# State-space loop of a small hybrid network: a step's two projections as one block product of seven half-width products, SiLU as one function, and the steps reordered

## The chip, the cores and the metric

The kernel runs on 1 core of one Trainium2 chip. The metric is the time of the kernel on the device in microseconds (us). A core has a matrix engine (TensorE, PE in the profile, with its weight loads as PEld), VectorE (DVE), ScalarE (ACT), GpSimd (POOL) and SyncE (SP), which here only issues transfers (DMA). TensorE writes into PSUM, which is split into eight banks of 512 float32 columns; the other data lie in SBUF, 128 partitions wide. All arithmetic that concerns us is in float32.

## The reference: what is computed

The input x has 2 batches of 512 tokens of width 512 (1024 tokens in eight tiles of 128). Six blocks follow each other: a gated feed-forward layer with 4-bit weights, a state-space layer, the feed-forward layer again, a small memory layer, attention, and the memory layer again. The change is in the state-space layer. Cut to what matters, with 128 heads of 64 channels, 8 groups of heads, 128 states, and chunks of 128 tokens:

```python
h = x * rsqrt(mean(x * x) + EPS) * norm_w
proj = einsum('bsd,od->bso', h, in_proj_w)          # 8192 gate, 8192 hid, 1024 B, 1024 C, 128 dt
gate, hBC, dt = split(proj)
hBC = silu(causal_conv(hBC, conv_w, conv_b))        # four taps along the tokens, by channel
hid, B, C = split(hBC)
dt = softplus(dt + dt_bias); A = -exp(A_log)
# by chunk: M = (C . B) * exp(segsum(A * dt)); Y_diag = M @ (hid * dt)
# states carried from chunk to chunk; Y_off = (C * exp(cumsum)) . state before the chunk
y = Y_diag + Y_off + Dp * hid
yg = y * silu(gate)
yg = yg * rsqrt(mean over the group (yg * yg) + EPS) * gnorm_w
out = x + einsum('bsd,od->bso', yg, out_proj_w)
```

## The kernel before

**The steps.** The 8192 channels are taken 128 at a time (two heads, one "pair"), for one batch of 512 tokens. A group of heads has 8 pairs. A step is (g, b, q): group, batch, pair in the group; b changes after eight q, g after both b. So there are 128 steps, and the loop in `ssm` calls `period(n)` for n = 0 to 129. One period works on three steps at once: the projections and convolution of step n (`cur`), the state-space sums of step n-1 (`p1`), and the output projection of step n-2 (`p2`).

**What one period does on TensorE, by its name in the profile and its line:** the projection of hid, cp_h, four products of 128 x 128 by 128 x 512 (L883, called from `period`); the chunks' states st of p1 (L1078); the output product po of p2, four chunks into four PSUM banks that add up over the eight q (L1000); py of p1, the products with M (L1160) and with the carried states (L1169); the gate's projection pg (L883); and ht, four transposes of hid (L1213). In the trace a float32 product counts as two instructions.

**The other engines.** VectorE: the taps 2 to 4 of the convolution (`conv_taps`, L897), the product with SiLU's second half (`silu`, L906: SiLU is built as (tanh(x/2) + 1) * x, with the convolution's weights halved beforehand), hc = hid * dt (L1021), two scans that make the decays within a chunk (L974, one for each head), their product with C·B (L988), the carried states (L1088), and yg (L1176, L1180). ScalarE: first tap (L892), Tanh of hid (L902) and of the gate (L1017), six scalings hd (L1029), two Exp over the scans (L979, L1125), the square of yg (L1186), the scaling of the output weights (L1191). GpSimd: Cs, C times the decay since the chunk's start (L990, 768 columns), and the sum of squares ssum (L1187).

**Work that comes once in eight steps.** B and C of the next group or batch are projected and convolved at q = 5 and q = 6 (`group_b`, `group_c`), B is transposed into Btok (L945, L947) and C·B is formed (L954, L958). When a group and batch is through, pr (L1108) sums the squares over channels, ScalarE takes the root (L1113), and four chunks of po are scaled on ScalarE (L1148) and added to x on GpSimd (L1150). In periods 1 to 7 `setup_later` also prepares dt and the decays of batch 1.

**What sets the order.** Inside the loop the order on TensorE, VectorE, ScalarE and GpSimd is the order in which the program is written (`in_order`); SP's transfers are placed by the scheduler. The program waits wherever two engines touch the same tile; for a PSUM tile that holds for two readers as well. A bank that is used again waits for its last reader.

**PSUM in the loop:** four banks for po, and one each for "tr" (ht, then st, bt, cb, pr), "mm" (pg, B, C), "dd" (cp_h) and "y" (py).

**Transfers.** Weights of the projections are 256 KB tiles (128 x 512 float32) from a pool of 20; they are loaded at b = 0 and kept for b = 1. Each step loads rows, 1024 KB, the decays of two heads broadcast to all partitions (L966).

Of the kernel before, what the change touches and what calls it, by code (L numbers as in the profile page):

```python
# [18 lines left out]
P = 128  # L19
# [33 lines left out]
OT_HID, OT_B, OT_C, OT_DT = NPT, 2 * NPT, 2 * NPT + NG, 2 * NPT + 2 * NG  # L53
# [213 lines left out]
class Kernel:  # L267
    def __init__(self, tc, ctx, a, out):
# [13 lines left out]
        self.eps = self.const.tile([P, 2], F32, name="eps")  # L282
        nc.vector.memset(self.eps[:, 0:1], EPS)
        nc.vector.memset(self.eps[:, 1:2], 4.0 * EPS)
# [12 lines left out]
    def ssm_const(self):  # L297
        with (
            self.tc.tile_pool(name="ssm_const", bufs=1) as pool,
            self.tc.tile_pool(name="early", bufs=1) as self.early,  # L300
        ):
            self.sc = pool
            self.small = pool.tile([P, 80 * 5 + 2 * NPT + KD], F32, name="small")
            self.later = pool.tile([P, S], F32, name="later")
            self.bias = pool.tile([P, 2, NH], F32, name="bias")
            yield
# [30 lines left out]

    def w2(self, src, name):
# [5 lines left out]
    def norm_parts(self, tag, each=None, gain=None, lazy=False):  # L344
# [15 lines left out]
        def root(t, to):  # L360
            nc.scalar.activation(
                rstd[:, t:to], mv[:, t:to, 1], AF.Sqrt, bias=self.eps[:, 0:1]
# [57 lines left out]
    def unpack_in(self, pool, which, ht):  # L420
# [10 lines left out]
        wt = self.wpool.tile([P, KD, P], F32, tag="w", name=f"w{which}_{ht}")  # L431
# [4 lines left out]
        return wt  # L436
# [27 lines left out]
    def ffn(self, n, then=None, during=None):  # L464
# [10 lines left out]
        def weight(which, ht):  # L475
            if first:
                t = (
                    self.unpack_out(pool, ht)
                    if which == 2
                    else self.unpack_in(pool, which, ht)  # L480
                )
# [6 lines left out]
            load = self.w2 if which == 2 else self.w  # L488
# [18 lines left out]
        def sums(ht):  # L507


            w1, w3 = weight(1, ht), weight(3, ht)  # L510
            lo, hi = slice(0, 2), slice(2, 4)
            if ht:
                s, u = (
                    self.wpool.tile([P, KD, P], F32, tag="w", name=f"ws{i}{n}_{ht}")
                    for i in range(2)
                )
# [174 lines left out]
    def ssm(self, hT, start, turn):  # L691
        tc, nc = self.tc, self.nc
        self.hT, self.start, self.turn = hT, start, turn
        with ExitStack() as ctx:
            self.sp = ctx.enter_context(tc.tile_pool(name="ssm", bufs=1))
            ctx.enter_context(self.banks("psum_s", tr=1, po=4, dd=1, mm=1, y=1))
            ctx.enter_context(self.in_order())
            self.steps = [
                Step(g, b, q) for g in range(NG) for b in range(NB) for q in range(PAIRS)
            ]  # L700
            self.wo = {}
# [3 lines left out]
    def ssm_norm(self):  # L705
# [9 lines left out]
        nc.vector.tensor_scalar(  # L715
            out=small[:, :400], in0=small[:, :400], scalar1=0.5, scalar2=None, op0=ALU.mult
        )
        ms = self.sc.tile([P, NT], F32, name="ms")

        def each(t, h):  # L720
# [4 lines left out]
            nc.scalar.activation(m, m, AF.Sqrt, bias=self.eps[:, 0:1], scale=1.0 / D)  # L725
# [8 lines left out]
    def dt_z(self, b):  # L734
        nc, (z, e, o) = self.nc, self.zeo
        bs = slice(b * NC, (b + 1) * NC)
        pz = self.ps("y", [P, NC, NH], f"pz{b}")
# [84 lines left out]
    def ssm_setup(self, t, ht, hT):  # L822

        nc = self.nc
        if (t, ht) == (NC + 1, 1):
            self.hT = hT
            self.gw, self.sh, late = {}, {}, []
# [10 lines left out]
            self.wdt = self.w(self.a["w_in"][OT_DT], "wdt")  # L838
# [6 lines left out]
            for first, taps, end in late:  # L845
                first()
                taps()
                end()
        elif (t, ht) == (NC + 1, NHT - 1):
# [12 lines left out]
    def setup_later(self, n, part):  # L862


        for at, f, *args in (
# [5 lines left out]
            ((5, 2), self.decay, "start", "tr"),  # L871
            ((5, 3), self.row, 0, "tr"),
            ((6, 2), self.row, 1, "tr"),
            ((6, 3), self.decay, "dt_end", "tr"),
            ((7, 2), self.decay, "whole", "tr"),
# [12 lines left out]
    def first_tap(self, p, ct, name):  # L888

        w = self.convw[:, ct, :]  # L890
        acc = self.early.tile([P, S], F32, tag="acc", name=f"acc_{name}", bufs=2)
        self.nc.scalar.activation(acc, p, AF.Identity, bias=w[:, 4:5], scale=w[:, 3:4])  # L892
        return p, w, acc, name

    def conv_taps(self, p, w, acc, name):
        for s in range(1, 4):
            self.nc.vector.scalar_tensor_tensor(  # L897
                out=acc[:, s:], in0=p[:, : S - s], scalar=w[:, 3 - s : 4 - s],
                in1=acc[:, s:], op0=ALU.mult, op1=ALU.add,
            )  # L900
# [996 lines left out]
```

## Time and profile before

| | us |
|---|---|
| time, median of 3 runs | 2763.68 (2761.5 to 2764.07) |
| span of the profiled execution | 2762.9 |
| TensorE busy | 2683.4 |
| VectorE busy | 1999.1 |
| ScalarE busy | 1110.3 |
| GpSimd busy | 522.8 |

The profile is of one execution, whose own time is its span from the first to the last instruction; the three times are of other executions. A row of groups reads: line, engine, operation, tile written and tiles read, shape, how many; then busy us and mean ns of one; then the engine's idle time ahead of these instructions and what ended it. A timeline row reads: start in us, length in us, engine, line, operation, tiles, how many in a row; in brackets the idle time before it and its releaser. A waits row reads: who waited for whom, us in all, times, longest. An instruction's own length can hold a wait too: Cs is between 1.80 and 2.75 us long, a scan between 1.19 and 2.81.

The loop's ht transposes start at 258.3 us for the first step and at 2098.5 us at the last row of that line. In the window from 250 to 2107 us TensorE is busy for 1847 of 1857 us, VectorE for 1496, ScalarE for 830, GpSimd for 482; the granted clock is 1.00 and the DMA share 0.29.

### The profile page before, as it was taken

What the parts mean: (1) busy time and instruction counts of PE and PEld (TensorE: products, weight loads), DVE (VectorE), ACT (ScalarE), POOL (GpSimd) and SP (SyncE); (2) the same over time, 40 slices, a digit from 0 to 9 for tenths busy, and PEclk for the clock granted to TensorE, in tenths of its full rate; (3) what the DMA queues carried; (4) which work ended last, traced back from release to release, by engine and by line L of the source; (5) the groups of instructions that cost most, each with busy time, mean ns of one, the idle gap of its engine ahead of it and who ended that gap; (6) DMA issues with size and microseconds to landing.
All of it is one profiled execution on the core that took longest, in us unless ns stands there. A gap on an engine that the chain in (4) does not pass through costs nothing.

```text
span 2762.9 us, 33381 instructions
## 1 busy us (share of the span) xinstructions
PE 2683.4 (97%) x12208; PEld 1395.9 (51%) x12208; DVE 1999.1 (72%) x3622; ACT 1110.3 (40%) x2428; POOL 522.8 (19%) x344
## 2 busy tenths in 40 slices
PE   8999999999999999999999999999999999889897
PEld 4445555555555555555555555555555444445443
DVE  7845877878778788787878878778886532665555
ACT  2214443444444344444444434444443211344443
POOL 0001122323223222231322312323130000110000
PEclk9999999999999999999999999999999999889988
DMA  7623133223323322322332332232221110000000
GB/s 205 199 98 114 69 107 132 90 77 130 107 84 116 110 84 96 124 92 87 129 100 80 116 125 84 84 130 96 84 99 50 31 54 23 0 1 2 1 1 31
DMA packets 75619, 237.76 MB, mean 86 GB/s; under 512 B 9824, under 2 KB 10400, under 8 KB 58944
## 3 DMA queue, kind: packets, MB, share of 16 engines
q1 hardware_dynamic: 70416, 226.00, 23.9%
q10 hardware_dynamic: 4752, 8.65, 0.8%
q8 instruction: 97, 1.59, 0.2%
q0 software_dynamic: 288, 0.98, 0.1%
q14 instruction: 66, 0.54, 0.1%
HBM read 223.80 MB, written 11.80 MB: 85 GB/s over the span
## 4 chain that ended last, share of the span: by engine, by line
PE 86%; DVE 8%; ACT 4%; issue 1%; POOL 0%; DMA 0%; SPq 0%; ACTq 0%; DVEq 0%; POOLq 0%
PE po L1000 15%; PE pg L883 14%; PE cp_h L883 13%; PE fo L669 5%; PE fmm L502 5%; PE py L1160 4%; PE st L1078 3%; PE py L1169 3%; PE fy L502 2%; PE cp_CT L883 2%; PE cp_BT L883 2%; PE ht L1213 2%; DVE acc_h L897 1%; PE w L1667 1%; PE fdd L502 1%; PE av L1683 1%
## 5 line engine op out<-in xcount | busy, mean ns | idle before, releaser
L883 PE MATMUL pg<-hT_s,wi 128*128 128x512 f32 x1024 | 474.3, 606 | 0.0
L1000 PE MATMUL po<-wo,yg 128*128 128x512 f32 x1024 | 460.7, 593 | 0.5 <-DVE yg L1180 0.5
L883 PE MATMUL cp_h<-hT_s,wi 128*128 128x512 f32 x1024 | 460.6, 592 | 0.0
L974 DVE TENSOR_TENSOR_SCAN M<-rows,later 128x512 f32<-128x512 f32 x256 | 431.7, 1725 | 0.0
L1187 POOL TENSOR_TENSOR ssum<-ssum,sq 128x512 f32<-128x512 f32 x112 | 142.4, 1271 | 1215.7 <-ACT sq L1186 1215.7
L897 DVE SCALAR_TENSOR_TENSOR acc_h<-cp_h,small,acc_h 128x511 f32<-128x511 f32 (+2 forms) x384 | 286.4, 746 | 21.3 <-ACT acc_h L892 12.2
L883 PEld LDWEIGHTS pg<-hT_s,wi 128*128 128x128 f32 x1024 | 184.6, 190 | 206.8 <-issue 204.2
L1000 PEld LDWEIGHTS po<-wo,yg 128*128 128x128 f32 x1024 | 184.8, 190 | 184.4 <-issue 183.6
L883 PEld LDWEIGHTS cp_h<-hT_s,wi 128*128 128x128 f32 x1024 | 184.6, 190 | 183.6 <-issue 183.6
L990 POOL TENSOR_TENSOR Cs<-CT,rows 128x768 f32<-128x768 f32 x128 | 252.5, 1972 | 18.7 <-PE py L1169 16.0
L902 ACT ACTIVATE th_h<-acc_h 128x512 f32<-128x512 f32 x128 | 80.7, 630 | 348.3 <-DVE acc_h L897 342.6
L1029 ACT ACTIVATE hd<-ht,end 128x64 f32<-128x64 f32 x768 | 171.1, 324 | 44.5 <-DVE hc L1021 44.4
L1186 ACT ACTIVATE sq<-yg 128x512 f32<-128x512 f32 x112 | 70.6, 630 | 284.2 <-DVE yg L1180 284.2
L988 DVE TENSOR_TENSOR M<-M,CB 128x512 f32<-128x512 f32 x256 | 166.2, 686 | 12.4 <-ACT M L1125 12.3
L1021 DVE TENSOR_TENSOR hc<-ht,dt 128x512 f32<-128x512 f32 x128 | 88.1, 689 | 115.5 <-PE ht L1213 115.5
L1088 DVE SCALAR_TENSOR_TENSOR st<-st,whole,st 128x64 f32<-128x64 f32 x512 | 108.8, 274 | 65.5 <-ACT st L1083 65.5
L979 ACT ACTIVATE M<-M 128x512 f32<-128x512 f32 x128 | 80.7, 630 | 169.6 <-DVE M L974 169.6
L1631 DVE CUSTOM_DVE_ANT_0 j<-s,future 128x384 f32<-128x384 f32 (+3 forms) x256 | 112.8, 487 | 46.2 <-PE s L1621 46.0
L1160 PEld LDWEIGHTS py<-M,hc 128*64 128x64 f32 x2048 | 109.4, 136 | 68.2 <-issue 64.7
L1160 PE MATMUL py<-M,hc 128*64 128x128 f32 x2048 | 140.5, 279 | 1.1 <-DVE M L988 1.1
L1078 PEld LDWEIGHTS st<-hd,Btok 128*128 128x128 f32 x768 | 104.1, 191 | 69.7 <-issue 41.3
L906 DVE SCALAR_TENSOR_TENSOR v<-v,pg 128x512 f32<-128x512 f32 x128 | 87.3, 682 | 48.5 <-ACT v L1017 47.8
(330 smaller groups left out, 3762.1 us busy)
## 6 DMA issues: line engine op xcount, KB each, us to landing
rows<-rows SPq DMA_DIRECT2D x128, 1024.0 KB, 4.7
wi<-in_w_in_dram SPq DMA_DIRECT2D x144, 256.0 KB, 2.8
wo<-in_w_out_dram SPq DMA_DIRECT2D x64, 256.0 KB, 3.0
keep<-w ACTq DMA_DIRECT2D x33, 256.0 KB, 3.7
wk<-keep SPq DMA_DIRECT2D x33, 256.0 KB, 2.7
wi<-in_q_dram SPq DMA_DIRECT2D x44, 128.0 KB, 3.1
sc<-in_s_dram SPq DMA_DIRECT2D x44, 128.0 KB, 3.2
wi<-in_q_dram SPq DMA_DIRECT2D x11, 256.0 KB, 3.3
```

The source lines that it names most:

```text
L502: nc.tensor.matmul(dst, lhsT=w[:, k, :], rhs=x[:, k, :], start=start and k == 0, stop=stop and k == 1, skip_group_check=True,)
L669: nc.tensor.matmul(po, lhsT=act[ht][:, b, c * P : (c + 1) * P], rhs=w2[ht], start=ht == 0, stop=ht == NHT - 1,)
L883: self.nc.tensor.matmul(p, lhsT=wt[:, k, :], rhs=self.hT[b][:, k, :], start=k == 0, stop=k == KD - 1)
L897: self.nc.vector.scalar_tensor_tensor(out=acc[:, s:], in0=p[:, : S - s], scalar=w[:, 3 - s : 4 - s], in1=acc[:, s:], op0=ALU.mult, op1=ALU ...
L974: self.nc.vector.tensor_tensor_scan(out=m, data0=rows[:, i, 0, :], data1=self.later, initial=0.0, op0=ALU.add, op1=ALU.mult,)
L988: self.nc.vector.tensor_tensor(out=m, in0=m, in1=sh["CB"], op=ALU.mult)
L990: self.nc.gpsimd.tensor_tensor(out=cur.Cs, in0=sh["CT"][:, P:].unsqueeze(1).to_broadcast([P, 2, S - P]), in1=cur.rows[:, :, 1, P:], op=ALU ...
L1000: self.nc.tensor.matmul(self.po[c], lhsT=p2.yg[:, c * P : (c + 1) * P], rhs=self.wo[p2.ct], start=p2.q == 0, stop=p2.q == PAIRS - 1,)
L1029: nc.scalar.mul(hd[:, c, ch], p1.pt[:, c, ch], self.dec["dt_end"][:, b * NC + c, h0 + i : h0 + i + 1],)
L1078: nc.tensor.matmul(pst[:, c, :], lhsT=self.sh[p1.g, p1.b]["Btok"][:, c, :], rhs=hd[:, c, :], start=True, stop=True,)
L1160: nc.tensor.matmul(py[ch, cs], lhsT=hc[:, c, ch], rhs=p1.M[i].rearrange("p (c t) -> p c t", c=NC)[:, c, :], start=c == 0, stop=c == 0, ski ...
L1187: nc.gpsimd.tensor_tensor(out=self.ssum, in0=self.ssum, in1=sq, op=ALU.add)
```

## The change

**One product for both projections.** Of a step's 128 x 512 weights for the gate and 128 x 512 for hid, and of the 512 x 512 tile of normalised x, a 2 x 2 block product is made, [gate; hid] = W · H, where the blocks of W split the inner dimension and those of H split the inner dimension and the tokens (256 and 256). Strassen's manner (Winograd's variant) takes seven block products of 128 x 256 by 256 x 256, each two products on TensorE of 256 columns, in place of eight. They use sums of H's blocks (`mix`, once for each batch, kept in `mixed`) and sums of the step's weights (`add_up`, three additions on GpSimd for each b = 0 step). The sums are stored to DRAM (`keep_sums`) and loaded for b = 1; the weights are now loaded for both batches, as pairs of 512 KB from a pool of 6.

**Where the products go.** Three banks: X takes the two halves of hid, R the gate, G a copy of X's first product, onto which another product is added. Between products ScalarE copies X aside: into G, then into u twice. The gate comes as R minus u, on VectorE, in two halves of 256 columns. For the convolution of the second half, three columns are copied from G in front of X.

**SiLU** is one ScalarE function (Silu) over hid, gate, B and C, in place of Tanh and a VectorE product; the weights are no longer halved.

**The order of a step.** ht (of p1) now opens the period. Then X1 into X, R1 into R, the copy into G, G's product, X2; st; X3; one of the four po products; X4; py; R2; the other three po. rows is loaded one period earlier. ht, st and py share one bank, "t". The group's end takes its root at the end of period q = 1, and the four chunks of po are added to x on VectorE (`leave`) at the start of period q = 2. bt, cb and pr use bank X.

```diff
-            ctx.enter_context(self.banks("psum_s", tr=1, po=4, dd=1, mm=1, y=1))
+            ctx.enter_context(self.banks("psum_s", t=1, po=4, X=1, G=1, R=1))
...
+    def mix(self, b):
+        nc, h, m = self.nc, self.hT[b], self.mixed[b]
+        b11, b12 = h[:, 0:2, :HS], h[:, 0:2, HS:]
+        b21, b22 = h[:, 2:4, :HS], h[:, 2:4, HS:]
+        nc.vector.tensor_tensor(out=m[:, 0], in0=b11, in1=b12, op=ALU.subtract)
+        nc.vector.scalar_tensor_tensor(
+            out=m[:, 1], in0=m[:, 0], scalar=-1.0, in1=b22, op0=ALU.mult, op1=ALU.subtract
+        )
+        nc.vector.tensor_tensor(out=m[:, 2], in0=b12, in1=b22, op=ALU.subtract)
+        nc.vector.tensor_tensor(out=m[:, 3], in0=b21, in1=m[:, 1], op=ALU.add)
...
+    def add_up(self, st):
+        if st.b:
+            return
+        add, w, s = self.nc.gpsimd.tensor_tensor, st.w, st.ws
+        add(out=s[:, 0:2], in0=w[:, 0:1].to_broadcast([P, 2, 2, P]), in1=w[:, 1:3], op=ALU.add)
+        add(out=s[:, 2], in0=s[:, 0], in1=w[:, 2], op=ALU.add)
+        add(out=s[:, 3], in0=s[:, 2], in1=w[:, 3], op=ALU.add)
...
+    def leave(self, c, direct):
+        b, po, r = self.done
+        x = self.x[b * NC + c]
+        if direct:
+            nc.vector.scalar_tensor_tensor(
+                out=x, in0=po[c], scalar=r[:, c : c + 1], in1=x, op0=ALU.mult, op1=ALU.add
+            )
+            return
...
+    def product(self, dst, w, x, start=False, stop=False):
+        for k in range(2):
+            self.nc.tensor.matmul(
+                dst, lhsT=w[:, k, :], rhs=x[:, k, :],
+                start=start and k == 0, stop=stop and k == 1, skip_group_check=True,
+            )
...
     def period(self, n):
...
+            self.keep_sums(cur)
+            if nxt is not None:
+                self.load_rows(nxt)
+            if after is not None and q == PAIRS - 5:
+                self.fetch_bc(*after)
+            if at(n + 2) is not None:
+                self.fetch(at(n + 2))
+            if nxt is not None:
+                self.add_up(nxt)
...
+            for c in range(NC):
+                nc.tensor.transpose(pt[:, c, :], p1.hid[:, c * P : (c + 1) * P], self.ident)
...
+            self.product(X[:, V], w[:, 2], b11, start=True)
+            self.product(R[:, V], ws[:, 1], m[:, 2], start=True)
+            nc.scalar.copy(G[:, V], X[:, V])
+        if self.done is not None:
+            for c in range(NC):
+                self.leave(c, True)
...
+            self.product(G[:, V], w[:, 3], b21)
+            self.product(X[:, V], ws[:, 2], m[:, 1])
             if n > 0:
                 self.within(cur)
+            self.first_tap(cur.hid[:, :HS], G[:, V], ct)
+            nc.scalar.copy(u[:, 0], X[:, V])
...
+            for s in range(1, 4):
+                self.tap(cur.hid[:, s:HS], G[:, 4 : 4 + HS - s], ct, s)
...
+            self.product(X[:, V], ws[:, 0], m[:, 0])
+            nc.scalar.copy(u[:, 1], X[:, V])
+            nc.scalar.copy(X[:, 1:4], G[:, 1 + HS : 4 + HS])
         if p2 is not None:
+            self.gather(p2, 0)
         if cur is not None:
+            self.product(X[:, V], ws[:, 3], b22, stop=True)
+            nc.vector.tensor_tensor(out=v[:, HS:], in0=R[:, V], in1=u[:, 1], op=ALU.subtract)
             if n > 0:
+                self.decays(cur)
                 self.times_c(cur)
+                self.carried_c(cur)
...
+            self.first_tap(cur.hid[:, HS:], X[:, V], ct)
+            for s in range(1, 4):
+                self.tap(cur.hid[:, HS:], X[:, 4 - s : 4 + HS - s], ct, s)
+            self.product(R[:, V], w[:, 1], m[:, 3], stop=True)
+            nc.scalar.activation(cur.hid, cur.hid, AF.Silu)
...
+            nc.vector.tensor_tensor(out=v[:, :HS], in0=R[:, V], in1=u[:, 0], op=ALU.subtract)
...
+            nc.scalar.activation(v, v, AF.Silu)
...
+            self.gather(p2, *range(1, NC))
...
+        if after is not None and q == PAIRS - 2:
+            self.group_bt(*after)
+        if after is not None and q == PAIRS - 1:
+            self.group_cb(*after)
+        if p2 is not None and p2.q == PAIRS - 1:
+            self.group_norm(p2)
...
-        with k.ssm_const(), k.weights("a", 20, 12):
+        with k.ssm_const(), k.weights("a", 6, 12):
```

`decays` is the two Exp, `times_c` the two products with C·B on VectorE, `carried_c` Cs on GpSimd, `group_norm` pr with the root and its reciprocal. The feed-forward layers take their weights from the smaller pool in pairs and are otherwise as they were.

## The prediction

> **What bounds the kernel now.** I read the page from its first part down, then the chain, the groups by line, the waits, and the timeline of one step.
>
> ```profile
> PE 2683.4 (97%) x12208; PEld 1395.9 (51%) x12208; DVE 1999.1 (72%) x3622; ACT 1110.3 (40%) x2428; POOL 522.8 (19%) x344
> ...
> PE 86%; DVE 8%; ACT 4%; issue 1%; POOL 0%; DMA 0%; SPq 0%; ACTq 0%; DVEq 0%; POOLq 0%
> ...
> L883 PE MATMUL pg<-hT_s,wi 128*128 128x512 f32 x1024 | 474.3, 606 | 0.0
> L974 DVE TENSOR_TENSOR_SCAN M<-rows,later 128x512 f32<-128x512 f32 x256 | 431.7, 1725 | 0.0
> L897 DVE SCALAR_TENSOR_TENSOR acc_h<-cp_h,small,acc_h 128x511 f32<-128x511 f32 (+2 forms) x384 | 286.4, 746 | 21.3 <-ACT acc_h L892 12.2
> ```
>
> TensorE is busy 97% of the span and is 86% of the chain that ended last; pg has no idle time before it. In the timeline the state-space loop lies at 250 to 2107 us, and its 128 steps start (at their ht transposes) 13.28 or 13.29 us apart where nothing special is in them. The eight steps of a group and batch take 115.16 or 116.05 us by turns, 115.6 in the mean. That is pure TensorE: 13.29 x 8 = 106.3, B and C 2 x 3.44, C·B 1.03, pr 0.95, bt 0.33 make 115.5. So TensorE bounds the loop, and DVE stands second: 11.8 of 13.5 us in the step at 1226.
>
> Two more rows matter, since they show what DVE's 11.8 us hide. The timeline at 1413, cut to four lines:
>
> ```profile
> 1414.37 1.28 POOL L1187 TENSOR_TENSOR ssum<-ssum,sq 128x512 f32<-128x512 f32 x1 [13.51 <-ACT sq L1186]
> ...
> 1415.42 4.00 DVE L974 TENSOR_TENSOR_SCAN M<-rows,later 128x512 f32<-128x512 f32 x2
> 1415.60 2.74 POOL L990 TENSOR_TENSOR Cs<-CT,rows 128x768 f32<-128x768 f32 x1
> ```
>
> Two scans alone take 2.33 (the pair at 920.66, with no GpSimd operation beside it); here 4.00. The first waits until ssum ends (1415.64), runs 1.1; Cs, 1.81 when alone, goes next; the second scan follows it. So a scan, with two SBUF inputs, and a GpSimd operation take turns: **ssum's end + 3.78 = both scans done**.
>
> And from the waits view:
>
> ```profile
> ACT hd L1029 <- DVE hc L1021: 44.4, 66, 8.6
> ```
>
> hd and hc only read ht, yet hd waits for hc: the program keeps two engines off one PSUM tile in program order, reads too. The changed kernel, as built, does the same.
>
> **The change on TensorE.** pg takes eight issues in 3.44 us, 0.430 each; a half-width one is 0.215. The block product has 7 x 4 = 28 of them, 6.03 us in place of 6.89, if the weight loads stay hidden (st issues a load and a 128-column product every 0.128, so they should). A plain step becomes ht 0.44 + 6.03 + st 0.77 + po 3.45 + py 1.69 = 12.4, eight steps with the same 9.2 for B, C, C·B, pr and bt 108.4. Taken alone that is 16 x (115.6 − 108.4) = 115 us.
>
> **What it puts in their way.** Times count from a step's ht. X1 is issued 0.44 to 1.30, R1 to 2.16, G to 3.02, X2 to 3.88, st to 4.65, X3 to 5.51, one po to 6.37, X4 to 7.23, py to 8.92, R2 and three po to 12.4. Consumers see a result 0.2 after its last issue (ht 1249.15 to hc 1249.79).
>
> The new chain: ScalarE's three-column copy into X reads G, so it waits until VectorE's three taps on G are through; X4 writes X, so it waits for the copy. The taps stand behind both scans. No row has a 256-column tap; 64 columns take 0.274 (st, L1088) and 512 take 0.745, and a PSUM tensor-tensor falls from 0.69 at 512 to 0.424 at 256 (O, L1704). I take 0.48, from the line through 64 and 512; its bounds are 0.27 and 0.75, of which the fall from 0.69 to 0.424 leaves about 0.37 to 0.6 for the range. From both scans done (E): taps 1.42, copy 0.20 (the 128-column copy has 0.256), so X4 starts at E + 1.67, against 6.37 wanted: a stall of E − 4.7.
>
> And the chain closes on itself. After the copy ScalarE loads a table, since Silu and Exp alternate now: two loads a step in the built program, where before had 15 + 15 around Sqrt. ScalarE's timeline shows what one costs:
>
> ```profile
> 1203.61 0.26 ACT L1113 ACTIVATE r<-pr,eps 128x4 f32<-128x4 f32 x1 [1.53 <-PE pr L1108]
> 1203.89 1.28 ACT L1125 ACT_TABLE_LOAD   x1
> 1205.19 0.63 ACT L1125 ACTIVATE M<-M 128x512 f32<-128x512 f32 x1
> ```
>
> From r's end at 1203.87 to M's Exp it is 1.3 in all. Behind the copy and the load on ScalarE are queued both Exp, the first tap of X and Silu of hid; DVE's M·CB waits for the Exps, its taps on X for the first tap, yg stands behind these. From the first Exp to the end of the second M·CB it is 1.97 (Exp 0.63, a wait 0.05, M·CB 0.60 to the next and 0.69; the second Exp is through by 1.2), the taps on X 1.42, yg and yg·v 1.43, sq and ssum 2.03 (0.63 + 1.27, two waits): 6.85. The sum from one ssum's end to the next:
>
> 3.78 (scans, with Cs between) + 1.42 + 0.20 + 1.30 + 6.85 = **13.55 us** for batch 1.
>
> In batch 0 GpSimd first adds up the weights of the next step (512 + 256 + 256 columns; 1.27 for 512 by ssum), so only the first add, 1.05 net, stands between the scans: **13.0 us**. Neither sum holds TensorE: its 12.4 wait. Mean of a plain step 13.28, as before. Of the gain on TensorE nothing is left there.
>
> Silu of hid, which the next ht needs, ends 0.6 ahead of it, so it adds nothing; were ScalarE later by more than that, ht would stall. The SiLU steps saved on DVE (0.697 + 0.682) are spent on the split taps (six of 0.48 for three of 0.745) and two subtractions of 0.42: +0.1. ScalarE gains three copies of 256 columns (between 0.256 at 128 and 0.479 at 384, I take 0.37) and the loads, 3.7 a step on the 5.7 of the windows view at 1226: 9.4, under 12.4, so it hurts by order alone. A Silu row is not there; I take Tanh's 0.63 (0.59 to 0.76, the ScalarE rows of 512).
>
> The Trainium skill's "ScalarE: Activation LUTs", section "What ACT_TABLE_LOAD costs", speaks against this change harder than the rows: it puts a switch at about 2.66 us, 1.28 of load and 1.38 of drain. By it the loop would be 1.36 longer, 14.9 and 14.4, an estimate from that page. The row at 1203.89 shows 1.30 and no drain beside it.
>
> **The special steps,** stall beside TensorE's floor:
> - q=0: X1 waits for CB (0.69, after cb): 12.4 + 0.55 = 12.95.
> - q=1: pr at the end, and the loop's stall of 1.15 (batch 1) or 0.6: 14.5 or 13.95.
> - q=2: pr's bank is X, and the square root comes after yg, sq, silu of v and a load: X1 waits 1.4 or 2.0. Then four leaves (4 x 0.74, 2.7 net) now stand on DVE ahead of hc and the scans, where ScalarE and GpSimd did them: stall 1.45. 15.25 or 15.85.
> - q=3, 4: 13.55, or 13.05 in batch 0 (G's copy waits 0.05 for silu of v behind wo).
> - q=5, 6 have 3.44 more; q=5 keeps the stall: 17.0 or 16.45. In q=6 ssum ends early: 16.2 with bt, or 16.5 in batch 0, where GpSimd's sums for q=7 wait for the buffer that C's product frees, Cs behind them, and meet yg·v.
> - q=7: Btok's copy, on X, comes after C's taps (2.31 on DVE at the step's end) and its Silu: X1 waits 1.45. With cb 14.9 or 15.1.
>
> Sums: batch 1 117.9, batch 0 116.95 (12.95, 13.95, 15.85, 2 x 13.05, 16.45, 16.5, 15.1); mean 117.4. Against 115.6: +1.8, x 16 = **+29 us**. The DMAs grow by 64 x 0.5 MB for gate and hid of batch 1, and as much for sums stored and for sums loaded, 96 MB onto 238, at a DMA share of 0.29 in the loop. All are issued a step or two ahead on SP (0.33 an issue), rows a step earlier than now; stores of sums stand in front of them there and wait only for GpSimd's sums of the step before. Rows land in 4.7, a step is 13: nothing, hidden behind a step; if one came late, X1 would wait up to those 4.7. Set-up work of batch 1 moved to bank X, with Exp and Ln loads among Silu ones: some four loads of 1.3, +5. The feed-forward's smaller weight pool (6 pairs for 20 tiles): nothing, loads of 2.8 behind hidden tiles of about 6 us.
>
> 2762.9 (the profile's span; the median is 0.8 above) + 34 = **2797 us**.
>
> **Rivals.**
> - *The scans meet no GpSimd operation*, so that both are done 2.33 after hc and X4 isn't held up: plain steps fall to 12.4, q=1 and q=5 lose their stall too; 113.4 a group, 16 x (113.4 − 115.6) + 5 = −30: 2733. For: in before the DVE held 11.8 of 13.5 without hurting, and shorter taps (0.37, half of 0.745) would bring ssum forward. Against: ssum ends 2 us into a step by the sum above, after hc, so it must meet the scans. **Decides:** if ssum ends within 0.5 us of ht. 0.20.
> - *The whole of TensorE's gain*, no stalls at bank X either: 2650. Every X1 wait would have to be wrong. 0.04.
> - *Balance*: the loop 0.1 a step shorter and sqrt's wait half: within 0.2% (5.5 us, about what a measurement can tell): 0.08.
> - *Half-width products aren't half*, so the change does not do what it says: a load of 0.190 per 0.215 slips, at 0.25 an issue the seven products cost 7.0, TensorE 13.4 a step. Plain steps hardly change (the loop rules), q=0, 2, 5, 6, 7 gain 0.8 each: +64, 2861. 0.09.
> - *A table switch costs more than its load*: at most the 1.53 idle before r at 1203.61, which the trace puts down to pr; were it the load's, 1.5 on the five steps q=1 to 5, 16 x 7.5 = +120: 2917. 0.05.
>
> **How the numbers follow.** The forecast, ScalarE's, VectorE's and GpSimd's loop at 2765 to 2830, has 0.54. The first rival and the whole gain make faster 0.24; balance 0.08; the forecast and the last two slower 0.68. Taps between 0.37 and 0.6 move the loop by −0.7 to +0.7 in five steps of eight, −56 to +56; so 2730 to 2850 for 8 in 10, with the first rival's 2733 in it.
>
> **What would show it.** Plain steps 13.4 to 13.7 apart in batch 1, 12.9 to 13.2 in batch 0; TensorE idle 0.6 to 1.3 before X4 with the three-column copy as releaser; two table loads a step at 1.28; scan pairs near 3.8 after ssum; idle before X1 in q=2 and q=7. Steps at 12.4 refute the loop; matmul issues over 0.23 confirm the fourth rival; a gap after each load, the fifth.

## The result, and the profile after

| | before | after |
|---|---|---|
| time, median (lowest to highest), us | 2762.59 (2759.27 to 2764.07), 4 runs | 2838.03 (2837.18 to 2838.82), 4 runs |
| ratio to before, 95% interval | | 1.0279 (1.0265 to 1.0294) |
| span of the profiled execution | 2762.9 | 2836.0 |
| start to the first ht | 258.3 | 266.3 |
| first to last ht | 1839.8 | 1900.4 |
| after the last ht | 664.7 | 669.3 |

The change costs 75 us by the medians, 73 by the two spans, where 34 were forecast. Of all executions in this document two, one of run e15 and one of before beside it, ran in a slower state (3382.9 us at a mean granted clock of 0.745, 3960.5 at 0.65) and are left out of every time and ratio. The result has the sign, the loop that sets the plain steps, and nearly all the special steps that were forecast; one step in eight is far off. The page after, with the lines that answer those shown of before (busy us, the chain by engine, the groups):

```profile
PE 2650.7 (93%) x13744; PEld 1705.0 (60%) x13744; DVE 2048.9 (72%) x4040; ACT 1588.7 (56%) x3252; POOL 703.5 (25%) x476
...
PE 70%; DVE 22%; ACT 5%; issue 2%; POOL 0%; DMA 0%; ACTq 0%; SPq 0%; DVEq 0%; POOLq 0%
...
L1008 DVE TENSOR_TENSOR_SCAN M<-rows,later 128x512 f32<-128x512 f32 x256 | 437.1, 1746 | 0.0
...
L903 DVE SCALAR_TENSOR_TENSOR hid<-hid,small,hid 128x256 f32<-128x256 f32 (+3 forms) x768 | 366.7, 478 | 41.8 <-ACT hid L900 23.6
L1075 PE MATMUL hid<-hT_s,wgh 128*128 128x256 f32 x1024 | 289.4, 408 | 57.7 <-ACT r L1055 39.6
...
L1075 PE MATMUL hid<-hT_s,wsum 128*128 128x256 f32 x512 | 141.2, 398 | 38.4 <-ACT hid L1176 38.4
...
L1215 ACT ACT_TABLE_LOAD x128 | 164.2, 1283 | 2.3
L1016 ACT ACT_TABLE_LOAD x126 | 161.7, 1283 | 2.3
```

VectorE's part of the chain has gone from 8% to 22%. The products, which had no idle time ahead of them, now wait for the square root (r, L1055) and for the three-column copy (L1176). A 256-column tap takes 478 ns, the 0.48 that the prediction took. A plain step of batch 1 (q=4), by its timeline:

```profile
1395.25 0.60 PE L1107 MATMUL ht<-masks,hid 128*128 128x128 f32 x4
...
1395.80 1.26 POOL L1235 TENSOR_TENSOR ssum<-ssum,sq 128x512 f32<-128x512 f32 x1 [9.61 <-ACT sq L1234]
...
1396.49 4.34 DVE L1008 TENSOR_TENSOR_SCAN M<-rows,later 128x512 f32<-128x512 f32 x2
...
1397.02 2.73 POOL L1029 TENSOR_TENSOR Cs<-CT,rows 128x768 f32<-128x768 f32 x1
...
1400.76 1.48 DVE L903 SCALAR_TENSOR_TENSOR hid<-hid,small,hid 128x255 f32<-128x255 f32 x3
...
1402.33 0.15 ACT L1176 COPY hid<-hid 128x3 f32<-128x3 f32 x1 [1.02 <-DVE hid L903]
1402.49 1.28 ACT L1016 ACT_TABLE_LOAD   x1
...
1402.53 1.13 PE L1075 MATMUL hid<-hT_s,wsum 128*128 128x256 f32 x4 [0.77 <-ACT hid L1176]
...
1403.79 1.15 ACT L1016 ACTIVATE M<-M 128x512 f32<-128x512 f32 x2
...
1409.36 1.27 POOL L1235 TENSOR_TENSOR ssum<-ssum,sq 128x512 f32<-128x512 f32 x1 [9.61 <-ACT sq L1234]
```

This is the forecast chain in its order: ssum ends at 1397.06, the scans at 1400.83 (3.77 later; 3.78 was forecast), the taps, the copy, the load beside X4 (which starts after 0.77 of idle) and ahead of both Exp, and the next ssum ends at 1410.63, 13.57 after the first (13.55 was forecast).

hd still waits for hc, though both only read ht, as the waits view shows (us, times, longest):

```profile
ACT hd L1136 <- DVE hc L1129: 25.6, 19, 2.0
```

In q=2, where hc stands behind the leaves, it is 1.08 (at 1370.09).

Step by step (ht to next ht, us; typical values of steps past the set-up):

| step | batch 1: before, after, forecast | batch 0: before, after, forecast |
|---|---|---|
| q=0 | 13.6, 13.2, 12.95 | 13.3, 13.25, 12.95 |
| q=1 | 14.1, 14.4, 14.5 | 14.1, 13.8, 13.95 |
| **q=2** | **13.3, 17.8, 15.25** | **13.7, 17.7, 15.85** |
| q=3, 4 | 13.3, 13.56, 13.55 | 13.4 and 13.3, 13.0, 13.05 |
| q=5 | 16.7, 17.0, 17.0 | 16.7, 16.5, 16.45 |
| q=6 | 17.05, 16.3, 16.2 | 17.05, 16.4, 16.5 |
| q=7 | 14.2, 14.5, 14.9 | 14.2, 14.6, 15.1 |

q=2 alone is 2.6 and 1.9 over its forecast: 8 x (2.57 + 1.87) = 36 us, where 39 were missed by the spans. Its timeline in batch 1, just ahead of the step above:

```profile
1362.75 0.95 PE L1050 MATMUL pr<-masks,ssum 128*128 128x1 f32 x8
...
1363.56 0.64 PE L1107 MATMUL ht<-masks,hid 128*128 128x128 f32 x4
1363.78 0.63 ACT L1231 ACTIVATE ssum<-yg 128x512 f32<-128x512 f32 x1 [2.00 <-PE pr L1050]
1364.32 0.61 ACT L1242 ACTIVATE v<-v 128x512 f32<-128x512 f32 x1
1364.93 1.28 ACT L1055 ACT_TABLE_LOAD   x1
1366.23 0.26 ACT L1055 ACTIVATE r<-pr,eps 128x4 f32<-128x4 f32 x1
1366.53 0.18 DVE L1056 RECIPROCAL r<-r 128x4 f32<-128x4 f32 x1 [3.69 <-ACT r L1055]
...
1366.55 2.07 PE L1075 MATMUL hid<-hT_s,wgh 128*128 128x256 f32 x4 [2.35 <-ACT r L1055]
1366.74 2.73 DVE L1065 SCALAR_TENSOR_TENSOR x<-po,r,x 128x512 f32<-128x512 f32 x4
```

and the windows view of it (stretch, length; busy of PE, PEld, DVE, ACT, POOL; granted clock, DMA share, GB/s):

```profile
1363.50:1366.50 3.00, 0.69 (x6) 0.45 (x5) 0.00 (x0) 2.69 (x4) 0.00 (x0) 0.85 0.00 0
1366.50:1369.70 3.20, 3.15 (x8) 2.53 (x9) 3.14 (x6) 0.36 (x1) 0.00 (x0) 0.50 0.02 5
1369.70:1373.00 3.30, 3.30 (x10) 2.69 (x9) 2.94 (x4) 1.90 (x7) 0.00 (x0) 0.58 0.00 0
```

Three things stand here: ScalarE's square waits 2.00 for pr before it comes to the root; VectorE idles 3.69 at the reciprocal with all else of it queued behind; and X1 finds the granted clock at 0.50, so that the four issues of a block product (a row x4) take 1.9 in place of 1.03.

### The profile page after: what moved, and what is told of

It is laid out like the page before. It is cut to its first block, busy times and chain, and to the rows that moved or that the text cites. A ratio compares the mean times of both kernels' runs of the same rounds, so it can differ in the third digit from the quotient of the medians.

```text
span 2836.0 us, 38242 instructions
## 1 busy us (share of the span) xinstructions
PE 2650.7 (93%) x13744; PEld 1705.0 (60%) x13744; DVE 2048.9 (72%) x4040; ACT 1588.7 (56%) x3252; POOL 703.5 (25%) x476
## 4 chain that ended last, share of the span: by engine, by line
PE 70%; DVE 22%; ACT 5%; issue 2%; POOL 0%; DMA 0%; ACTq 0%; SPq 0%; DVEq 0%; POOLq 0%
PE hid L1075 13%; PE po L1039 11%; DVE M L1008 9%; PE gate L1075 6%; PE fmm L509 5%; PE fo L675 5%; PE py L1197 4%; DVE hid L903 4%; PE py L1205 3%; PE fy L509 2%; PE cp_BT L892 2%; PE cp_CT L892 2%; DVE hc L1129 2%; PE st L1156 2%; PE w L1731 1%
## 5 line engine op out<-in xcount | busy, mean ns | idle before, releaser
L903 DVE SCALAR_TENSOR_TENSOR hid<-hid,small,hid 128x256 f32<-128x256 f32 (+3 forms) x768 | 366.7, 478 | 41.8 <-ACT hid L900 23.6
L1075 PE MATMUL hid<-hT_s,wgh 128*128 128x256 f32 x1024 | 289.4, 408 | 57.7 <-ACT r L1055 39.6
L1075 PE MATMUL hid<-mixed,wsum 128*128 128x256 f32 x1024 | 273.6, 390 | 0.0
L1075 PEld LDWEIGHTS hid<-hT_s,wgh 128*128 128x128 f32 x1024 | 197.5, 203 | 93.9 <-ACT r L1055 43.2
L1075 PEld LDWEIGHTS hid<-mixed,wsum 128*128 128x128 f32 x1024 | 188.0, 193 | 22.1
L1075 PE MATMUL hid<-hT_s,wsum 128*128 128x256 f32 x512 | 141.2, 398 | 38.4 <-ACT hid L1176 38.4
L1075 PEld LDWEIGHTS hid<-hT_s,wsum 128*128 128x128 f32 x512 | 86.7, 189 | 137.7 <-ACT hid L1176 73.6
L900 ACT ACTIVATE hid<-hid,small 128x256 f32<-128x256 f32 x256 | 142.6, 557 | 20.1 <-PE hid L1075 7.7
L1075 PE MATMUL gate<-mixed,wsum 128*128 128x256 f32 x512 | 144.5, 408 | 0.9 <-DVE v L1225 0.9
L1075 PE MATMUL gate<-mixed,wgh 128*128 128x256 f32 x512 | 144.6, 405 | 0.0
```

The lines of the kernel that those rows point to most:

```text
L900: self.nc.scalar.activation(out, p, AF.Identity, bias=w[:, 4:5], scale=w[:, 3:4])
L903: self.nc.vector.scalar_tensor_tensor(out=out, in0=p, scalar=self.convw[:, ct, 3 - s : 4 - s], in1=out, op0=ALU.mult, op1=ALU.add,)
L1075: self.nc.tensor.matmul(dst, lhsT=w[:, k, :], rhs=x[:, k, :], start=start and k == 0, stop=stop and k == 1, skip_group_check=True,)
```

## The experiments

Each time is a median with its ratio to before on the same chip, 95% interval; e11 to e13 ran on a second chip and e14 on a third (before there: 2764.0 and 2764.8), so compare the ratios. Step lengths are of one profiled execution each. Edits are against the changed kernel where nothing else is said.

### The loop: three links cut one at a time

Run e1, the copy's wait:

```
+ nc.scalar.copy(side[:, :3], G[:, 1 + HS : 4 + HS])
  self.first_tap(cur.hid[:, :HS], G[:, V], ct)
  ...
- nc.scalar.copy(X[:, 1:4], G[:, 1 + HS : 4 + HS])
+ nc.scalar.copy(X[:, 1:4], side[:, :3])
```

> The three columns of G that X needs are copied to a small SBUF tile as soon as G's product is done, ahead of the first tap, and from there into X; so the copy into X no longer waits for the three taps on G, and X4 no longer waits for it. The loop theory (ssum's end, scans in turns with GpSimd, taps on G, copy, table load, Exp, products with CB, taps on X, yg, ssum): the copy, the load and the Exps then run beside VectorE's taps, and what is left of the loop is VectorE's own order: 3.78 + 1.42 + st 0.85 + v 0.42 + 1.29 + 1.42 + 1.43 + 2.03 = 12.6 in batch 1 and about 12.1, so TensorE's 12.4, in batch 0. Plain steps go from 13.56 and 13.0 to 12.65 and 12.4; five steps of eight gain 0.9 or 0.6, 16 x 3.75 = 60: about 2778. The rival, that the scans are late whatever X4 does and the step is set by VectorE's and GpSimd's turns alone: plain steps keep 13.56 and 13.0 and the time stays within 10 of 2838.

Run e2, the loads (all three Silu of the loop, those of B and C included):

```
- activation(..., AF.Silu)
+ activation(..., AF.Tanh)
```

> The three Silu of the loop become Tanh, which shares a table with Exp, so that the two table loads of each step go (the function computed is another one; every instruction and every wait is otherwise the same). The loop theory has one of the two loads on its path, 1.3: plain steps fall from 13.56 and 13.0 to TensorE's floor of 12.4, five of eight steps gain 1.15 or 0.6, 16 x 4.4 = 70, and the set-up loses some of its loads too: 2760 to 2770. The rival, that ScalarE has time enough (56% busy) and the loads lie in its idle time: no change, 2838.

Run e3, GpSimd's turn:

```
- nc.gpsimd.tensor_tensor(out=self.ssum, in0=self.ssum, in1=sq, op=ALU.add)
```

> GpSimd's addition to ssum is left out (the sum of squares then holds one pair of heads only), so that no GpSimd operation ends two us into a step. The loop theory: the scans go at 2.33 right after hc, X4 is not held up, plain steps are TensorE's 12.4 in both batches, two table loads a step notwithstanding; 16 x 4.4 = 70 less, about 2768. The rival, that the table loads alone set the step and the turn-taking of VectorE and GpSimd is beside it: plain steps stay over 13, 2820 to 2838.

| run | time | ratio | q=4, batch 1 | q=4, batch 0 |
|---|---|---|---|---|
| after | 2838.0 | 1.0279 (1.0265 to 1.0294) | 13.56 | 13.03 |
| e1 | 2803.7 | 1.0150 (1.0133 to 1.0167) | 12.70 | 12.65 |
| e2 | 2798.9 | 1.0133 (1.0115 to 1.0152) | 12.57 | 13.06 |
| e3 | 2820.4 | 1.0204 (1.0177 to 1.0232) | 12.57 | 13.09 |

In batch 1 each of the three cuts takes q=4 to within 0.13 of TensorE's floor, so copy, load and ssum do lie on one loop. The floor itself shows as 12.57 (12.4 was forecast). q=3 stands directly behind q=2 and begins with its delay: 12.57 in e3, 13.12 in e1, and still 13.56 in e2, where ssum ends 1.81 behind ht as in the changed kernel.

In batch 0 q=4 falls in e1 alone. That does not take load and ssum off the loop there. In the changed kernel the forecast path closes in batch 0 too:

```profile
1275.96 1.28 POOL L1235 TENSOR_TENSOR ssum<-ssum,sq 128x512 f32<-128x512 f32 x1 [5.43 <-ACT sq L1234]
...
1276.72 3.75 DVE L1008 TENSOR_TENSOR_SCAN M<-rows,later 128x512 f32<-128x512 f32 x2
...
1277.19 2.19 POOL L985 TENSOR_TENSOR wsum<-wgh 128x512 f32<-128x512 f32 x1
...
1289.00 1.28 POOL L1235 TENSOR_TENSOR ssum<-ssum,sq 128x512 f32<-128x512 f32 x1 [5.43 <-ACT sq L1234]
```

ssum ends at 1277.24, the scans with GpSimd's first add between them at 1280.47, 3.23 later (3.78 less 0.55 in the forecast), and the next ssum ends 13.04 after this one. Without the load (e2) ssum does come 0.65 earlier in q=4, but then GpSimd goes on to the first add of the weights at once, which now has its turn ahead of the scans, with the second add between them:

```profile
1256.93 1.27 POOL L1235 TENSOR_TENSOR ssum<-ssum,sq 128x512 f32<-128x512 f32 x1 [4.77 <-ACT sq L1234]
...
1257.09 0.60 PE L1107 MATMUL ht<-masks,hid 128*128 128x128 f32 x4
...
1258.16 1.27 POOL L985 TENSOR_TENSOR wsum<-wgh 128x512 f32<-128x512 f32 x1
...
1258.34 3.78 DVE L1008 TENSOR_TENSOR_SCAN M<-rows,later 128x512 f32<-128x512 f32 x2
...
1259.51 1.52 POOL L986 TENSOR_TENSOR wsum<-wsum,wgh 128x256 f32<-128x256 f32 x1
...
1269.44 1.28 POOL L1235 TENSOR_TENSOR ssum<-ssum,sq 128x512 f32<-128x512 f32 x1 [5.03 <-ACT sq L1234]
...
1271.40 3.22 DVE L1008 TENSOR_TENSOR_SCAN M<-rows,later 128x512 f32<-128x512 f32 x2
```

The scans end 5.03 behind ht, where they ended 4.99 behind it before, so X4 is as late as it was (0.30 of idle, 0.27 before); that the two agree is chance. One step on, ssum ends 0.57 behind ht (1270.72, ht at 1270.15) and the scans 4.47: q=5 of batch 0 takes 16.07 in place of 16.46, and q=1 falls likewise from 13.84 to 13.44. In e3 the adds run ahead into the step before, and Cs (1270.75 to 1272.57) has its turn ahead of the first scan: the scans end 5.05 behind ht in q=3, 4 and 5.

So the gains stay below the forecasts. e1 gained 34 in place of 60: q=3 of batch 1 fell by half only, batch 0 by 0.4 a step (its floor is 12.57), and q=2 of batch 0 took 0.8 more. e2 gained 39 in place of 70: q=3 in both batches and q=4 of batch 0 gave nothing. e3 gained 18 in place of 70: batch 0 gave nothing but in q=1, and its q=7 took 2.1 more, which was not followed up.

### The table loads where TensorE bounds

Run e6, the kernel before with SiLU as one function (four places; the halved weights and the norm's factor of four undone):

```
- nc.scalar.activation(v, p1.pg, AF.Tanh, scale=0.5)
- self.silu(v, v, p1.pg)
+ nc.scalar.activation(v, p1.pg, AF.Silu)
```

> The kernel before with SiLU as one ScalarE function and nothing else of the change (weights and the norm's constant not halved and quadrupled any more): VectorE loses two operations of 0.69 a step, ScalarE gains two table loads of 1.28 a step. Theory: TensorE bounds the kernel before, ScalarE is 40% busy and goes to about 60%, so the loads lie in its idle time: 2758 to 2768, within 0.2% of before. Rival: the loads stand on a path that TensorE waits for, as in the changed kernel, and a step grows by one load, 128 x 1.3 = 166, about 2930; a part of that if only some steps have no room.

2771.9, ratio 1.0037 (1.0024 to 1.0050): 9 us over before, 4 over the upper end of the theory. Plain steps keep 13.29 exactly; q=2 takes 14.29 (batch 0) and 13.68 in place of 13.72 and 13.29, 8 x 0.96 = 7.7. There Silu's load stands ahead of the four scalings of po on ScalarE, and in batch 0 TensorE's st waits 0.74 for hd behind them. VectorE's 150 us less bought nothing. So of the change's parts SiLU as one function costs 0.4% by itself, and more only where its load stands in a loop.

### q=2: clock, order on VectorE, order on ScalarE

Run e5, work for TensorE in the gap:

```
+ if self.done is not None:
+     for _ in range(2):
+         self.product(R[:, V], w[:, 2], b11, start=True)
  self.product(X[:, V], w[:, 2], b11, start=True)
```

> In the step after next to a group's end (q=2), two extra half-width products are issued into R between ht and X1, so that TensorE works (1.7 us) in the 2.35 us in which X1 waits for the square root; R's first product overwrites them. Theory: the granted clock falls to 0.50 from 1366.5 to 1373 because TensorE idled before, which holds G and the taps up; with the fill the clock stays at 1.0, the first four products take 1.03 each in place of 1.9, G is done 2.5 earlier, and X4, which then waits for the four leaves, hc, the scans and the taps on VectorE, starts 1.25 earlier: 16 x 1.25 = 20 less, 2818. Rival, that the four products are slow for another reason (their operands, a port shared with VectorE's leaves): the clock's row stays at 0.50, no gain, 2838 or a little more.

2827.8, ratio 1.0237 (1.0220 to 1.0254): 10 less, half of what was expected, with the clock as the theory has it. The same stretch of q=2 (from ht on):

```profile
1358.90:1361.90 3.00, 2.43 (x14) 1.87 (x14) 0.00 (x0) 2.70 (x4) 0.00 (x0) 1.00 0.00 0
1361.90:1363.80 1.90, 1.85 (x9) 1.64 (x10) 1.83 (x4) 0.36 (x1) 0.00 (x0) 1.00 0.00 0
```

X1 waits for the root as before, but the clock stays at 1.00, and q=2 takes 16.73 in all eight groups of batch 1 (17.8 in the mean after) and 17.41 in batch 0 (17.7). So idleness brings the clock down, and that is worth 1.1 and 0.3 a step; 16.73 is still 1.5 over the forecast. With the clock out of the way this run also shows where the step loses time behind X1: st waits 1.22 for hd, and hd waits for hc, which stands behind the leaves.

Runs e7 and e9, the leaves behind hc and the scans as shown; e9 also takes bank G for pr, `self.ps("G", ...)` in place of `self.ps("X", ...)`. (In e9 and in e10 below pr in G also changes what G holds in q=2, so that they compute another hid in that step; the instructions and waits are those of the edit.)

```
- for c in range(NC):
-     self.leave(c, True)
  ...
  self.within(cur)
+ for c in range(NC):
+     self.leave(c, True)
```

> Changed kernel, in the step q=2 the four leaves (output times root, added to x, on VectorE) come after hc and the two scans instead of ahead of them. Two things are late there side by side: VectorE (root, leaves, hc, scans, taps on G) and TensorE (X1 waits for the root, then four products at half clock, G ready only 5.5 after X1). Theory that both are late together: taking VectorE's order away alone gains at most 0.5 a step of q=2, 16 x 0.5 = 8, 2830 to 2838, since G is late by the clock. Rival, that VectorE's order alone sets it: X4 starts 3.5 earlier, 16 x 3.5 = 56, about 2782.

> As the run before, and the column sums pr for the root are written to bank G in place of X, so that X1 and R1 of q=2 no longer wait for the root, and only G's copy does. TensorE then idles about 1.0 in place of 2.4 to 3 us there. If the idle time is what brings the clock to 0.50, it stays at 1.0, G is ready 4 us earlier, VectorE's hc and scans are done before the root, leaves and taps follow at once and X4 starts 3.8 earlier: q=2 takes about 14 in place of 16.7 to 18.2, 16 x 3.8 = 61, about 2777. If the clock falls all the same, the gain is 1 to 2 a step of q=2, 2805 to 2820.

e7: 2840.1, ratio 1.0281 (1.0265 to 1.0298), no step changed, as the theory of two late things has it. e9: 2843.8, ratio 1.0297 (1.0278 to 1.0317), where 2777 was expected: my theory of q=2 fell there (q=2 takes 18.2 and 18.9). X1 and R1 no longer wait, but:

```profile
1369.01 0.18 DVE L1056 RECIPROCAL r<-r 128x4 f32<-128x4 f32 x1 [3.70 <-ACT r L1055]
1369.11 0.66 DVE L1125 TENSOR_TENSOR hc<-ht,dt 128x512 f32<-128x512 f32 x1
...
1371.93 2.70 DVE L1065 SCALAR_TENSOR_TENSOR x<-po,r,x 128x512 f32<-128x512 f32 x4
...
1376.34 1.52 PE L1075 MATMUL hid<-hT_s,wsum 128*128 128x256 f32 x4 [2.45 <-ACT hid L1176]
```

The reciprocal stands in VectorE's order at the end of q=1, so hc and the scans wait for the root wherever the leaves are put. I had looked at the leaves and not at the one short instruction ahead of them. The leaves now delay the taps, TensorE idles 2.45 ahead of X4 in place of X1, and the clock falls there (X4 takes 1.52).

Run e10, the edits of e1 and e9 together:

> The first experiment's edit (three columns copied early to SBUF) and the two of the run before together. The gains lie in different steps (plain ones and q=2), so they should add: 2804 less 61, about 2743, under the kernel before by 0.7%. If q=2 only hands its lateness on to the next steps (VectorE has 14.6 us of work in it), half of the 61 is left: 2770.

2786.1, ratio 1.0096 (1.0070 to 1.0121): 18 less than e1, but over both times that were expected, 2743 and 2770. With the early copy X4 waits for no tap and the gap of 2.45 ahead of it is gone; py now waits 2.08 in its place, and q=2 takes 16.1 and 17.1.

Runs e11, e12, e13: the root (`root`, the Sqrt) and its reciprocal (`over`) moved too, in q=2 alone; leaves 2 and 3 come behind the first half of v, and R1 no longer comes ahead of the copy. e12 adds e1's edit, e13 bank R for bt with R1 behind X2 in q=7.

```
- pr = self.ps("X", [P, NC], f"pr{p2.n}")
+ pr = self.ps("R", [P, NC], f"pr{p2.n}")
  ...
  nc.scalar.copy(G[:, V], X[:, V])
+ self.root()
  ...
  self.product(X[:, V], ws[:, 2], m[:, 1])
+ self.product(R[:, V], ws[:, 1], m[:, 2], start=True)
  self.within(cur)
+ self.over()
+ self.leave(0, True)
+ self.leave(1, True)
```

> Only the step q=2 of the changed kernel is mended: pr goes to bank R, R1 of that step is issued after X2, the square root comes behind ScalarE's copy into G, and the reciprocal and the leaves come behind hc and the scans on VectorE (two leaves ahead of the taps on G, two behind the first v). So far VectorE stood 3.7 us at the reciprocal, which waits for the root, with hc, the scans and hd's wait for hc behind it; that is what kept the two runs with late leaves slow. Theory: with nothing behind the root but the leaves, q=2 falls from 17.7 to about 14 (st is late by 1.05, VectorE has 14.6 us of work), 16 x 3.8 = 60 less than 2838, about 2777, and the granted clock rises to 0.985 or more. Rival, that the root and four leaves cost this step their time wherever they stand: q=2 stays over 16.5, 2820 or more.

> The mended q=2 of the run before, with the first experiment's early copy of G's three columns. Plain steps are then TensorE's 12.65 but for 13.1 in one of them, q=2 about 14: 2804 less 16 x 3.9 = 62, about 2741, that is 0.8% faster than the kernel before. Rival, that VectorE's work of q=2 comes back in q=3: half of the 62, 2773.

> As the run before, and the transposes bt of a group's B go to bank R, with R1 after X2 in q=7 too, so that X1 of q=7 no longer waits for Btok's copy (14.6 a step, where the floor with C times B is 13.6). G's copy still stands behind Btok's on ScalarE, so 0.5 to 0.9 of the 1.0 goes: 16 x 0.7 = 11 less than the run before. Rival, that G's copy is the later wait: no change.

| run | time | ratio | q=1, b1 and b0 | q=2, b1 and b0 |
|---|---|---|---|---|
| after | 2838.0 | 1.0279 (1.0265 to 1.0294) | 14.4, 13.8 | 17.8, 17.7 |
| e11 | 2797.2 | 1.0115 (1.0096 to 1.0133) | 14.7, 15.3 | 13.5, 14.3 |
| e12 | 2758.4 | 0.9980 (0.9968 to 0.9992) | 13.9, 15.3 | 13.6, 14.2 |
| e13 | 2760.5 | 0.9983 (0.9972 to 0.9995) | 13.9, 15.3 | 13.6, 14.9 |

q=2 falls by 4.3 and 3.4, as the theory has it, and with the early copy the gains add: e12 is 0.2% below the kernel before. Most of the rest of what was expected went into q=1 of batch 0, 1.4 longer than in the changed kernel (e11) and 1.9 longer than in e1 (e12), by a wait that I had made; in e12:

```profile
1206.07 0.41 DVE L1242 TENSOR_TENSOR v<-gate,u 128x256 f32<-128x256 f32 x1
1206.62 1.02 PE L1050 MATMUL pr<-masks,ssum 128*128 128x1 f32 x8 [1.58 <-DVE v L1242]
```

pr in bank R waits for R's last reader, v, which stands behind yg. bt in bank R (e13) took q=7 from 14.4 and 14.6 to 14.1 and 14.2, and gave it back in q=2 of batch 0 and in the set-up: no change. Run e14 puts that v ahead of yg in q=1 of e12's version.

> The root and side copy version, and in q=1 the first half of v (R minus u, VectorE) comes ahead of the two products that make yg. There pr, now in bank R, waited 1.58 us for that v in batch 0, which took q=1 from 13.5 to 15.3. Theory: pr then waits no more, q=1 of batch 0 falls by 1.5, 8 x 1.5 = 12 less, about 2746, 0.6% faster than the kernel before. Rival, that yg, 0.42 later, holds ssum and the next step by as much as pr gains: no change, 2758.

2750.3, ratio 0.9949 (0.9936 to 0.9963), q=1 of batch 0 at 13.8: the step falls by 1.5 as the theory has it, and the time by 8 of the 12 us.

Two runs for the 1.5 us that e5 had left open, with a second buffer for ssum:

```
- self.ssum = sp.tile(..., tag="ssum", bufs=1)
+ self.ssum = sp.tile(..., tag="ssum", bufs=2)
```

> Changed kernel with two buffers for ssum and nothing else. In q=1 of batch 1 ScalarE's square of the new group's first yg writes the one ssum buffer, so it waits until pr has read the old sum (2.00 idle behind pr), and Silu of v, the table load and the square root stand behind it. Theory: with two buffers the square starts 1.15 earlier, the root too, X1 waits 1.2 in place of 2.35, and a gap of that length leaves the granted clock at 1.0: q=2 of batch 1 falls by 1.1 and by another 1.1 of clock, to about 15.5; batch 0, where yg is late by itself, hardly moves: 8 x 2.2 = 18 less than 2838, about 2820. Rival, that the root is late by the load and Silu alone: no change.

> The mended version (root late, early copy, v first in q=1) with two buffers for ssum. There the root stands behind G's copy and only the leaves wait for it, so the square's wait for pr should be hidden: no change, 2746 to 2752. Rival, that ScalarE's queue in q=2 still holds hd and so st: up to 1.1 in batch 1's q=2, 9 less, 2741.

e15: 2827.3, ratio 1.0236 (1.0219 to 1.0252), where 2820 was expected; its profiled execution is the fastest of the five, span 2819.9. q=2 of batch 1 takes 15.6, where the forecast had 15.25; batch 0 stays at 17.9.

```profile
1356.60 0.63 ACT L1231 ACTIVATE ssum<-yg 128x512 f32<-128x512 f32 x1 [0.75 <-DVE yg L1223]
1356.82 0.95 PE L1050 MATMUL pr<-masks,ssum 128*128 128x1 f32 x8
...
1359.07 0.26 ACT L1055 ACTIVATE r<-pr,eps 128x4 f32<-128x4 f32 x1
...
1359.38 1.87 PE L1075 MATMUL hid<-hT_s,wgh 128*128 128x256 f32 x4 [1.12 <-ACT r L1055]
```

The square now starts ahead of pr, and X1 waits 1.12 in place of 2.35. So in batch 1 1.2 of the wait is the square's wait for the one buffer; Silu and the load account for no more than the 1.12 that is left. e16: 2748.0, ratio 0.9950 (0.9937 to 0.9963), the same as e14: once nothing but the leaves waits for the root, the buffer costs nothing.

## Why the prediction was wrong in size

**Right.** Half-width products are half (X1 at 1395.68, R1 at 1396.55: 0.87 for four issues). The tap at 0.48, the table load at 1.28, the scans' 3.78 behind ssum, and the closed loops: 13.55 in batch 1, measured 13.57 from ssum to ssum, and 13.0 in batch 0, measured 13.04. No gap stands behind a load: it ends at 1403.77 and Exp starts at 1403.79. The steps q=1, 3, 4, 5, 6 are all within 0.15. The transfers cost nothing, as forecast: DMA is 0% of the chain at 342.9 MB.

On the Trainium skill's page "ScalarE: Activation LUTs", section "What ACT_TABLE_LOAD costs", the trace goes with the 1.28 of load and shows no drain behind it. By its 2.66 a switch plain steps would have been 14.9, an estimate.

**Wrong: the term of q=2, "X1 waits 1.4 or 2.0" and with the leaves "15.25 or 15.85"**, measured 17.8 and 17.7. In it,
- the root in batch 1 was put "after yg, sq, silu of v and a load", and the square's wait for pr on the one ssum buffer was left out: X1 waits 2.35 and not 1.4 (e15: 1.12 once it is gone, and 15.6);
- in batch 0 X1 waits 2.97 and not 2.0; e15 brings it to 2.88 only. There yg itself is late in q=1, where GpSimd's sums of weights run beside the products with C·B: the pair of products takes 2.40 at 1239.70, where it takes 1.29 in batch 1, and yg ends 0.08 behind the next ht in place of 1.06 ahead of it. That 1.11 is enough for the 0.97 that X1 waits longer. The prediction had a meeting with these sums, of yg·v, for q=6 only. No run took the meeting away, so this cause is argued;
- the leaves' "stall 1.45" was counted through the scans to X4. Without the clock (e5) the step loses 1.8 or 1.9 behind X1, and most of it at st, which waits 1.22 for hd and hc behind the leaves;
- the granted clock was left out: 1.1 and 0.3 a step, 11 us (e5: 10).

With the floor's 0.17 these add up to the 2.57 of batch 1 (0.95 + 0.36 + 1.09 + 0.17) and the 1.87 of batch 0 (0.97 + 0.42 + 0.31 + 0.17).

**Mis-sized, smaller.** TensorE's floor: 12.57 for 12.4. Start and set-up, "+5": the eighth ht comes 9.7 later than before (382.2 against 372.5). The stretch after the last ht, for which no term stood: 4.6 longer. Between the kernels made from the changed one it varies from 665.8 (e12) to 673.4 (e9), and it goes with the time at half clock in it: 78.1 us in e12, 89.4 in e9, 84.6 in the changed kernel, 81.1 before. What sets that time was not tested.

Sum, by the spans: 34 + 36 (q=2) + 5 (set-up) + 4.6 (the end) − 6 (q=7 and q=1 shorter than forecast, q=0 longer, and what the typical values leave) = 73, rounded.

**Rivals.** "The scans meet no GpSimd operation" was the wrong way to a faster kernel, since they do meet; but the plain steps that it promised, 12.4, nearly come when the copy no longer waits (12.70 and 12.65 in q=4 of e1). Between these two kernels the order of the work decides: with the same products and the same loads e14 is 0.5% faster than before and the changed kernel 2.8% slower.

## What to carry to other kernels

An instruction that waits is priced with all that is queued behind it on its own engine: a reciprocal of 0.18 us held hc, the scans and the taps of a step for 3.7. When work is taken off the bounding engine, look for the loops that close between the other engines. Before cutting a link, ask which operation moves into its place: in batch 0 the scans ended 5.0 behind ht with the load and without it, since another add of GpSimd's had its turn first. And when a late chain is moved to another bank, count that bank's last reader too (pr, 1.58 behind v).

## What the runs showed that was not expected

The granted clock in q=2 comes in pieces. Added up over each step of the changed kernel, half clock lasts 0, 3.41 or 6.83 us and nothing between; the step takes 16.73, 16.91 and 18.0 to 18.2 in batch 1. The gap ahead of X1 is 2.35 in all of them. In each trace all the starts of half clock lie whole multiples of 3.413 us apart, whatever the program does in between.

This goes with the fixed window that runs free of the program, of about 3.4 us, of the Trainium skill's "TensorE: Matmul & The Clock Gate", section "What's actually happening". That page's section "Why this matters for your kernels" puts the limit at gaps of about 3 us.

Here a shorter one is enough: in e15 a gap of 1.12, behind pr's one-column products (0.95) and ht, brought 3.41 us of half clock in three of eight groups. Yet e5's gaps of 0.63 and 1.14 ahead of X1, e14's of 0.45 and 1.05, and e10's of 1.02 and 2.08 in one step brought none, so the length of a gap does not decide. Cut at those multiples of 3.413 us, the loops of all traces, past the set-up, show what does go with it, if pr and ht are counted as idle: every full-clock window with more than 2.41 us of idle TensorE was followed by half clock, and none with less than 2.11 was. In the changed kernel the border lies between 2.10 and 2.18, and e10 has no window over 1.85. No run set out to test this.
